# Layer 0: column biases' two row tiles on different output partitions, the tokens' statistics first, and the first unit's preparation last in banks of its own

## The chip, the cores and the metric

One Trainium2 chip, of which the kernel uses one core. A core has TensorE (PE, whose weight loads are listed apart as PEld), VectorE (DVE), ScalarE (ACT), GpSimd (POOL) and SyncE (SP, which only issues transfers). PSUM, where TensorE writes, has 128 partitions and 8 banks of 512 fp32 numbers for each partition; SBUF is the other on-chip memory. The metric is the time of one execution on the device in microseconds; the time of a kernel is the median of its runs. The engines run side by side, each working off its own queue in order; a semaphore holds an instruction until what it reads is there.

## The reference, cut to what matters

Four layers work one after the other on x of shape (2, 64, 64, 128). The change is in layer 0, an attention over all 4096 places of an image with four heads of 32 numbers and a relative position bias by row and by column:

```python
def _gn(v, G=32, eps=1e-5):          # each image, groups of 4 channels
    ...
    return ((g - m) / jnp.sqrt(s + eps)).reshape(v.shape)

def _L0_conv_ref(x, w_qkv, pos_emb_h, pos_emb_w):
    ...
    qkv = jnp.einsum('bhwc,cd->bhwd', x, w_qkv)
    q, k, v = jnp.split(qkv, [qk_dims, 2 * qk_dims], axis=-1)
    ...
    pos = relative_position_bias(pos_q, pos_emb_h, pos_emb_w).reshape(B, nh, L, L)
    scores = jnp.einsum('bnqd,bnkd->bnqk', q, k) * scale + pos
    attn = jax.nn.softmax(scores, axis=-1)
    out = jnp.einsum('bnqk,bnkd->bnqd', attn, v)
    ...

x = x + _L0_conv_ref(_gn(x), L0_conv_w_qkv, L0_conv_pos_emb_h, L0_conv_pos_emb_w)
```

`rel_logits_1d` gives for each query the product with the 64 embeddings of the possible distances in a row (`pos_emb_w`), and the same for columns of the image (`pos_emb_h`). All numbers are fp32. Layers 1 to 3 (a gated triangle product, an attention, two mixtures of experts) are not touched.

## The kernel before, in words

The whole image pair stays in SBUF as `self.x`, 64 blocks of 128 places by 128 channels, 32 blocks (`NC`) for each of the two images (`b`). Eight transfers of 512 KB, all on SP's queue, load it (L51 to L52).

**The start of layer 0** (`layer0`, L257). ACT's queue fetches `w_qkv` (L264) and then the two tables of position embeddings into `raw` (L282). POOL copies one-hot rows into the keys' tile `ka` (`l0_hot`, L499). In the order of the program there follow:

1. The tables: TensorE transposes them (L286), DVE and ACT copy each to four places of `pe` (L289).
2. A bound on the scores, from Gram matrices of the weights (L306, L320), the tables' norms and, later, the longest token: a chain of small DVE and TensorE instructions up to L354.
3. For each image `group_block` eight times (four transposes L113, `bn_stats` on DVE L116, a copy to `xT` on ACT L118), then `group_stats` (L125 to L105: aggregate, two tiny matmuls, a reciprocal root), then `xT` scaled by DVE in two halves (L395).
4. `lengths` for each half image: a Square (on ACT, L375, for the first half and on POOL, L373, for the second), four matmuls (L378), a maximum on DVE (L385). Between them stand `pieces(4)`: four steps of the first unit's preparation each time.
5. The verdict whether the bound is at most 60 (`tops`, L402 to L408, `at_most`, L248), which all engines read for the branch.
6. The rest of the first unit's preparation, and `l0_values` of image 0 (L484 and L491): eight groups of four matmuls, each copied to `v` by ACT.

All PSUM tiles of this part come from one tag, `misc`, with five banks. The tile framework lays down a fixed order for each engine when the program is built; it starts from the order of the program and may bring forward what its own estimate takes for ready.

**The loop** (`l0_bounded`, L503; the branch taken here). There are eight units: image, pair of heads, half of the queries. A unit has 4 query blocks of 512 by 32 key blocks. One turn makes the scores of a key block by four matmuls (L615, eight in the trace, since a matmul on fp32 shows as two records), their exponential on ACT (L623), the values of two turns earlier (L573), and the product with the column biases' exponentials `ew` on DVE (L626). After every second turn `piece()` takes one step of a generator, so a unit has 64 places for steps. In them run the finishing steps of the last query block (`l0_finish`, three steps each) and `l0_prepare` of the next unit. `more()` does the same at other places for the statistics of the next layer. Here the tag `misc` has two banks.

**The preparation of a unit** (`l0_prepare`, L639) is a generator whose every `yield` ends a step:

- queries: two projections (L657) into PSUM, each copied by ACT and DVE to six places of `qa` (L677 to L687); 5 steps for each projection, 10 in all;
- column biases: four groups `g`; in each, eight rows by two row tiles of the array (input partitions 32 to 63 and 96 to 127) make 16 matmuls, 32 records (L701). The right operand is `qa[..., y::S]`, every 64th number. Each row tile has a PSUM bank of its own (`pw[0]`, `pw[1]`), and both write partitions 0 to 63. ACT takes the exponential of each bank (L712) into the lower half of `ew`, and one transfer of 1 MB on SP's queue (L715) copies that to the upper half; 8 steps;
- row biases: four groups of 16 matmuls (L723), two row tiles (input partitions 0 to 31 and 64 to 95) writing partitions 0 to 63 and 64 to 127 of one bank; two copies by ACT and two by DVE for each group (L734); 4 steps;
- in the first half of a pair also the keys: four projections (L657), eight copies by ACT (L747) and eight by DVE (L748); 4 steps.

That is 26 steps for a unit with keys and 22 without.

## Time and profile before

The kernel's time is 4788.5 us (median of 4 runs, 4786.6 to 4790.2). The profiled execution took 4790.6 us, of which 4788.8 are the span from its first to its last instruction.

| stretch, us from the span's start | PE busy | DVE busy | ACT busy | granted clock |
|---|---|---|---|---|
| whole span, 4788.8 | 93% | 61% | 56% | 0.961 |
| start of layer 0, 0 to 88.36 | 55.31 | 44.36 | 49.45 | 0.77 |
| loop of layer 0, 88.36 to 2086.00 | 1959.24 | 1418.19 | 1239.42 | 1.00 |

The rows that the change and its neighbours touch, for the whole span:

| line and engine | instructions | mean or median of one, ns |
|---|---|---|
| L615 PE scores | 8192 | 595 |
| L573 PE values into the output | 8192 | 592 |
| L701 PE column biases | 1024 | 283 |
| L723 PE row biases | 1024 | 217 |
| L491 ACT copies of the values | 16 | 586 |

Busy time is a union of what overlaps: several matmuls on different tiles of the array run at the same time, so that mean times count is more than busy time. An engine's busy share over the whole span says little here, because the start and the loop have different limits; the stretches are to be read one by one. The granted clock is the share of TensorE's full clock that the throttle allowed.

### The profile page before, as it was taken

What the parts mean: (1) busy time and instruction counts of PE and PEld (TensorE: products, weight loads), DVE (VectorE), ACT (ScalarE), POOL (GpSimd) and SP (SyncE); (2) the same over time, 40 slices, a digit from 0 to 9 for tenths busy, and PEclk for the clock granted to TensorE, in tenths of its full rate; (3) what the DMA queues carried; (4) which work ended last, traced back from release to release, by engine and by line L of the source; (5) the groups of instructions that cost most, each with busy time, mean ns of one, the idle gap of its engine ahead of it and who ended that gap; (6) DMA issues with size and microseconds to landing.
All of it is one profiled execution on the core that took longest, in us unless ns stands there. A gap on an engine that the chain in (4) does not pass through costs nothing.

```text
span 4788.8 us, 76270 instructions
## 1 busy us (share of the span) xinstructions
PE 4473.5 (93%) x32236; PEld 1745.9 (36%) x32236; DVE 2943.8 (61%) x4850; ACT 2696.0 (56%) x3157; POOL 945.6 (20%) x848
## 2 busy tenths in 40 slices
PE   6999999999999999977899999999967999999999
PEld 3333333333333333335323233222235444444444
DVE  5676767677766767766755657555564444444447
ACT  5666565656666665545666766676731444333326
POOL 1000000000000000014455555555521000000008
PEclk8999999999999999988999999999977999999999
DMA  1000000000000000000000000000034000000001
GB/s 47 10 1 10 1 10 1 10 1 1 10 1 10 1 12 1 1 5 21 5 1 1 1 1 1 1 1 1 1 109 181 1 0 0 0 1 0 0 1 36
DMA packets 42562, 60.16 MB, mean 13 GB/s; under 512 B 4224, under 2 KB 24928, under 8 KB 41568
## 3 DMA queue, kind: packets, MB, share of 16 engines
q1 hardware_dynamic: 40912, 54.34, 3.7%
q8 instruction: 257, 4.21, 0.4%
q10 hardware_dynamic: 1296, 0.82, 0.1%
q14 instruction: 97, 0.79, 0.1%
HBM read 42.56 MB, written 4.19 MB: 10 GB/s over the span
## 4 chain that ended last, share of the span: by engine, by line
PE 76%; DVE 10%; ACT 7%; issue 3%; POOL 3%; DMA 0%; SPq 0%; ACTq 0%; POOLq 0%; DVEq 0%
PE l0o L573 16%; PE l0sc L615 16%; PE scl L2126 9%; PE oTl L2085 9%; PE l2sc L1498 5%; PE l2pos L1245 5%; PE l2av L1544 3%; PE f3ex L2235 2%; DVE l2es L1518 2%; POOL l2es L1521 2%; ACT l0es L623 2%; ACT l2es L1529 1%; DVE l0es L626 1%; PE l0pw L701 1%; PE l1p L988 1%
## 5 line engine op out<-in xcount | busy, mean ns | idle before, releaser
L626 DVE TENSOR_TENSOR l0es<-l0es,l0qe 128x1024 f32<-128x1024 f32 x1024 | 1250.3, 1228 | 529.4 <-ACT l0es L623 528.3
L623 ACT ACTIVATE l0es<-l0sc 128x1024 f32<-128x1024 f32 x1024 | 1043.3, 1024 | 605.0 <-PE l0sc L615 599.1
L573 PE MATMUL l0o<-l0es,l0v 64*33 64x512 f32 x8192 | 1072.8, 592 | 32.5 <-DVE l0es L626 17.0
L615 PE MATMUL l0sc<-l0qe,ka 64*64 64x512 f32 x8192 | 1079.6, 595 | 5.6 <-ACT l0es L623 5.0
L1529 ACT ACTIVATE l2es<-l2es 128x1024 f32<-128x1024 f32 (+3 forms) x576 | 559.1, 984 | 264.8 <-POOL l2es L1521 257.9
L1521 POOL TENSOR_TENSOR l2es<-l2es 128x1024 f32<-128x1024 f32 (+3 forms) x352 | 581.2, 1662 | 496.8 <-DVE l2es L1518 430.4
L2093 DVE TENSOR_TENSOR accl<-accl,esl 128x1024 f32<-128x1024 f32 x240 | 302.6, 1261 | 424.9 <-ACT esl L2137 421.2
L1518 DVE TENSOR_SCALAR l2es<-l2sc 128x1024 f32<-128x1024 f32 (+3 forms) x320 | 338.9, 1059 | 313.1 <-PE l2sc L1498 312.7
L2137 ACT ACTIVATE esl<-scl 128x1024 f32<-128x1024 f32 x240 | 245.6, 1023 | 485.2 <-PE scl L2126 451.8
L615 PEld LDWEIGHTS l0sc<-l0qe,ka 64*64 64x64 f32 x8192 | 298.5, 133 | 568.0 <-issue 490.2
L573 PEld LDWEIGHTS l0o<-l0es,l0v 64*33 64x33 f32 x8192 | 255.3, 108 | 646.4 <-issue 517.4
L2126 PE MATMUL scl<-l3qT,l3kT 128*128 128x512 f32 x1024 | 487.8, 596 | 0.0
L1498 PE MATMUL l2sc<-l2q,kept 32*128 32x512 f32 (+3 forms) x2304 | 390.9, 621 | 86.8 <-ACT l2es L1509 62.5
L2085 PE MATMUL oTl<-esl,l3v 128*128 128x512 f32 x960 | 451.1, 592 | 0.0
L776 POOL TENSOR_TENSOR x<-x,l0y 128x256 f32<-128x256 f32 x32 | 23.4, 731 | 1994.3 <-DVE l0y L771 1900.0
L1544 PE MATMUL l2av<-l2es,kept 128*32 128x512 f32 (+3 forms) x2304 | 310.0, 588 | 0.0
L1245 PE MATMUL l2pos<-kept 128*32 128x512 f32 x2416 | 296.6, 599 | 0.1
L2126 PEld LDWEIGHTS scl<-l3qT,l3kT 128*128 128x128 f32 x1024 | 188.3, 191 | 207.7 <-issue 191.5
L2085 PEld LDWEIGHTS oTl<-esl,l3v 128*128 128x128 f32 x960 | 181.7, 190 | 225.6 <-issue 222.5
L1509 ACT ACTIVATE l2es<-l2sc 128x1024 f32<-128x1024 f32 x224 | 226.2, 1010 | 54.4 <-PE l2sc L1498 53.0
L1498 PEld LDWEIGHTS l2sc<-l2q,kept 32*128 32x128 f32 x2304 | 116.6, 187 | 331.2 <-ACT l2es L1509 162.7
L1245 PEld LDWEIGHTS l2pos<-kept 128*32 128x32 f32 x2416 | 78.3, 111 | 174.8 <-issue 174.0
(707 smaller groups left out, 3763.2 us busy)
## 6 DMA issues: line engine op xcount, KB each, us to landing
f2w<-in_L_ffn_weight_dram SPq DMA_DIRECT2D x32, 1024.0 KB, 12.9
l0qe<-l0qe SPq DMA_DIRECT2D x8, 1024.0 KB, 6.7
x<-in_x_dram SPq DMA_DIRECT2D x8, 512.0 KB, 8.9
out_dram<-x SPq DMA_DIRECT2D x16, 256.0 KB, 2.3
kept<-in_L_attn_pos_rev_dram SPq DMA_DIRECT2D x1, 1792.0 KB, 6.5
ew<-in_L_ffn_expert_w_dram SPq DMA_DIRECT2D x1, 512.0 KB, 4.1
kept<-in_L_attn_pos_rev_dram SPq DMA_DIRECT2D x1, 256.0 KB
f2b<-in_L_ffn_weight_dram ACTq DMA_DIRECT2D x2, 128.0 KB, 2.8
```

The source lines that it names most:

```text
L573: nc.tensor.matmul(o[64 * h : 64 * h + HD + 1, r, :], lhsT=v1[rows, k, 2 * pair + h, :], rhs=es[rows, h, :], start=(k == 0), stop=(k == NC ...
L615: nc.tensor.matmul(sc[64 * c : 64 * c + 64, h, :], lhsT=ka[rows, k0 : k0 + 64], rhs=qa[rows, k // (NC // 2), qs], start=True, stop=True,)
L623: nc.scalar.activation(es, sc, AF.Exp)
L626: nc.vector.tensor_tensor(es, es, ew[:, :, qs], ALU.mult)
L1245: nc.tensor.matmul(out[part], lhsT=lhsT[:, part], rhs=rhs, start=start, stop=stop)
L1498: nc.tensor.matmul(sc[:, h2, off:], lhsT=kT[hs, k * P : (k + 1) * P], rhs=q[hs, off:], start=True, stop=True,)
L1518: nc.vector.tensor_scalar(es[:, :, lo:], sc[:, :, lo:], root, None, ALU.mult)
L1521: nc.gpsimd.tensor_tensor(part, part, part, ALU.mult)
L1529: nc.scalar.activation(es[:, :, off:], es[:, :, off:], AF.Silu)
L1544: nc.tensor.matmul(avs[i][hs, off:], lhsT=v[:, k, hs], rhs=es[h // 2][:, h % 2, off:], start=(k == 0), stop=last,)
L2085: nc.tensor.matmul(oT, lhsT=vs[b][:, k, :], rhs=es[:, i, :], start=(k == 0), stop=(k == NC - 1),)
L2126: nc.tensor.matmul(sc[:, i, :], lhsT=kTs[b][:, k * P : (k + 1) * P], rhs=qT[:, qb * 512 : (qb + 1) * 512], start=True, stop=True,)
```

## The change

- Two of the eight x transfers, blocks 32 to 47 (the first half of image 1), move from SP's queue to ACT's, where they are issued before `w_qkv`. `raw` moves to the weights' pool, and its two transfers are issued right after `w_qkv`.
- A local function `normed(b)` does the group blocks, the statistics and the scaling of one image. `normed(0)` stands before the tables and the bound, `normed(1)` between the `lengths` of image 0 and of image 1. Image 1's second Square goes from POOL to ACT.
- The first unit's preparation is no longer taken in pieces: it follows whole after the verdict, and it and `l0_values` use a tag `first`. The pool has four banks for each tag, eight in all, instead of five for one.
- In `l0_values` every second copy goes to DVE, for image 1 too, whose values are made inside the loop.
- In `l0_prepare`, for all units, the two row tiles of the column biases write partitions 0 to 63 and 64 to 127 of one bank. The row biases' copies have one more `yield` in each group, and the keys' copies one more in each projection: 34 steps with keys and 26 without.

```diff
@@ -49,7 +49,8 @@
         self.x = self.const.tile([P, B * NC, C], F32, tag="x", name="x")
         src = ins["x"].rearrange("b h w c -> (b h w) c").rearrange("(g p) c -> p g c", p=P)
         for g in range(0, B * NC, 8):
-            nc.sync.dma_start(out=self.x[:, g : g + 8, :], in_=src[:, g : g + 8, :])
+            queue = nc.scalar if g in (NC, NC + 8) else nc.sync
+            queue.dma_start(out=self.x[:, g : g + 8, :], in_=src[:, g : g + 8, :])
 
         self.ident = self.const.tile([P, P], F32, tag="ident", name="ident")
         make_identity(nc, self.ident)
@@ -262,6 +263,10 @@
             wp = st.enter_context(tc.tile_pool(reuse_waits="tile", name="l0w", bufs=1))
             w = wp.tile([P, 3 * C], F32, tag="wqkv", name="wqkv")
             nc.scalar.dma_start(out=w, in_=ins["L0_conv_w_qkv"])
+            raw = wp.tile([P, 2, HD], F32, tag="raw", name="l0raw")
+            nc.vector.memset(raw, 0.0)
+            for i, n in enumerate("hw"):
+                nc.scalar.dma_start(out=raw[: 2 * S - 1, i, :], in_=ins[f"L0_conv_pos_emb_{n}"])
 
 
             pe = wp.tile([P, 2, 2 * S - 1], F32, tag="pe", name="l0pe")
@@ -274,14 +279,18 @@
             v = wp.tile([P, NC, NH, HD + 1], F32, tag="v1", name="l0v1")
             with (
                 tc.tile_pool(reuse_waits="tile", name="l0s", bufs=2) as ap,
-                tc.tile_pool(reuse_waits="tile", name="l0sp", bufs=5, space=PSUM) as ps,
+                tc.tile_pool(reuse_waits="tile", name="l0sp", bufs=4, space=PSUM) as ps,
             ):
-                raw = ap.tile([P, 2, HD], F32, tag="raw", name="l0raw")
-                nc.vector.memset(raw, 0.0)
+                def normed(b):
+                    for g in range(NC // 4):
+                        self.group_block(ps, gst[:, b], b, g, xT[:, b, :])
+                    gm, gr = self.group_stats(ps, gst[:, b], b)
+                    for half in range(2):
+                        part = xT[:, b, half * 2048 : (half + 1) * 2048]
+                        nc.vector.tensor_scalar(part, part, gm, gr, ALU.subtract, ALU.mult)
+
+                normed(0)
                 for i, n in enumerate("hw"):
-                    nc.scalar.dma_start(
-                        out=raw[: 2 * S - 1, i, :], in_=ins[f"L0_conv_pos_emb_{n}"]
-                    )
                     pt = ps.tile([P, 512], F32, tag="misc", name=f"l0pe{n}")
                     nc.tensor.transpose(pt[:HD, :P], raw[:, i, :], self.ident)
                     for lo in range(0, P, 32):
@@ -357,19 +366,10 @@
                 nc.vector.memset(ones, 1.0)
                 most = ap.tile([P, 4], F32, tag="most", name="l0most")
                 nc.vector.memset(v[:, :, :, HD:], 1.0)
-                made = {}
-                first = self.l0_prepare(
-                    ps, (0, 0, 0), xT, w, pe, [ka], (qe[:, 0], qe[:, 1]), made
-                )
-
-                def pieces(n):
-                    for _ in range(n):
-                        next(first, None)
-
                 def lengths(b, half):
                     part = xT[:, b, half * 2048 : (half + 1) * 2048]
                     sq = ap.tile([P, 2048], F32, tag="sq", name=f"l0sq{b}_{half}")
-                    if half:
+                    if half and b == 0:
                         nc.gpsimd.tensor_tensor(sq, part, part, ALU.mult)
                     else:
                         nc.scalar.activation(sq, part, AF.Square)
@@ -387,15 +387,9 @@
                     )
 
                 for b in range(B):
-                    for g in range(NC // 4):
-                        self.group_block(ps, gst[:, b], b, g, xT[:, b, :])
-                    gm, gr = self.group_stats(ps, gst[:, b], b)
+                    if b:
+                        normed(b)
                     for half in range(2):
-                        part = xT[:, b, half * 2048 : (half + 1) * 2048]
-                        nc.vector.tensor_scalar(part, part, gm, gr, ALU.subtract, ALU.mult)
-                for b in range(B):
-                    for half in range(2):
-                        pieces(4)
                         lengths(b, half)
                 top = self.tops(ps, "l0", [most])
                 s1 = self.small.tile([1, 1], F32, tag="bs1", name="l0s1")
@@ -408,9 +402,11 @@
                     s1, s2, float(HD) ** -0.5, s1, ALU.mult, ALU.add
                 )
                 small = self.at_most("l0", s1, 60.0)
-                for _ in first:
+                for _ in self.l0_prepare(
+                    ps, (0, 0, 0), xT, w, pe, [ka], (qe[:, 0], qe[:, 1]), {}, tag="first"
+                ):
                     pass
-                self.l0_values(ps, 0, xT, w, v)
+                self.l0_values(ps, 0, xT, w, v, tag="first")
             with tc.If(small > 0) as fits:
                 self.l0_bounded(xT, w, pe, gst, na, nb, qe, ka, v)
             with fits.Else():
@@ -475,11 +471,11 @@
             nc.tensor.transpose(pt[:, k * P : (k + 1) * P], xT[:, at : at + P], self.ident)
         nc.scalar.activation(xT[:, blk], pt, AF.Identity, bias=nb, scale=na)
 
-    def l0_values(self, ps, b, xT, w, v, ones=False):
+    def l0_values(self, ps, b, xT, w, v, tag="misc"):
 
         nc = self.nc
         for g in range(NC // 4):
-            pv = ps.tile([P, 4, C], F32, tag="misc", name=f"l0pv{b}_{g}_{ones}")
+            pv = ps.tile([P, 4, C], F32, tag=tag, name=f"l0pv{b}_{g}")
             for i in range(4):
                 nc.tensor.matmul(
                     pv[:, i, :],
@@ -488,7 +484,7 @@
                     start=True,
                     stop=True,
                 )
-            nc.scalar.copy(
+            (nc.vector.tensor_copy if g % 2 else nc.scalar.copy)(
                 v[:, 4 * g : 4 * g + 4, :, :HD],
                 pv.rearrange("p i (h d) -> p i h d", d=HD),
             )
@@ -636,7 +632,7 @@
             while extra:
                 more()
 
-    def l0_prepare(self, ps, unit, xT, w, pe, kas, place, made):
+    def l0_prepare(self, ps, unit, xT, w, pe, kas, place, made, tag="misc"):
 
 
 
@@ -652,7 +648,7 @@
 
         def projected(j, g, name):
 
-            out = ps.tile([P, 512], F32, tag="misc", name=name)
+            out = ps.tile([P, 512], F32, tag=tag, name=name)
             for i in range(2):
                 nc.tensor.matmul(
                     out[64 * i : 64 * i + 64, :],
@@ -691,15 +687,12 @@
         for g in range(4):
 
 
-            pw = [
-                ps.tile([P, 8, 2, S // 2], F32, tag="misc", name=f"l0pw{t}_{g}_{i}")
-                for i in range(2)
-            ]
+            pw = ps.tile([P, 8, 2, S // 2], F32, tag=tag, name=f"l0pw{t}_{g}")
             for n in range(8):
                 for i, lo in ((0, 32), (1, 96)):
                     y = 32 * i + 8 * g + n
                     nc.tensor.matmul(
-                        pw[i][:S, n, :, :],
+                        pw[64 * i : 64 * i + S, n, :, :],
                         lhsT=pe[lo : lo + HD, 1, S - 1 - y : 2 * S - 1 - y],
                         rhs=qa[lo : lo + HD, :, y::S],
                         start=True,
@@ -709,13 +702,13 @@
             for i in range(2):
                 y = 32 * i + 8 * g
                 dst = ew[:S].rearrange("p h (x y) -> p y h x", y=S)
-                nc.scalar.activation(dst[:, y : y + 8], pw[i][:S], AF.Exp)
+                nc.scalar.activation(dst[:, y : y + 8], pw[64 * i : 64 * i + S], AF.Exp)
             yield
 
         nc.sync.dma_start(out=ew[S:], in_=ew[:S])
         for g in range(4):
 
-            ph = ps.tile([P, 8, S], F32, tag="misc", name=f"l0ph{t}_{g}")
+            ph = ps.tile([P, 8, S], F32, tag=tag, name=f"l0ph{t}_{g}")
             for i in range(8):
                 row = 8 * g + i
                 at = S - 1 - (half * (S // 2) + row)
@@ -730,6 +723,8 @@
             yield
             cols = slice(g * 512, (g + 1) * 512)
             for lo in (0, 64):
+                if lo:
+                    yield
                 for kh, copy in ((0, nc.scalar.copy), (1, nc.vector.tensor_copy)):
                     copy(
                         qa[lo + 32 : lo + 64, kh, cols].rearrange("p (x y) -> p x y", y=S),
@@ -740,8 +735,8 @@
             root = float(HD) ** -0.5
             for g in range(0, L // 512, 2):
                 pk = projected(1, g, f"l0pk{b}_{pair}_{g}")
-                yield
                 for i in range(2):
+                    yield
                     cols = slice((g + i) * 512, (g + i + 1) * 512)
                     lo = 64 * i
                     nc.scalar.activation(ka[:HD, cols], pk[lo : lo + HD], AF.Copy, scale=root)
```

## The prediction

> **What bounds the kernel now.** I read the page first (TensorE is busy for 93% of the span), then the chain of waits in order of time, the timeline of the first 90 us, the busy time by stretch, and last the column-bias line L701 beside its twin L723. The change touches layer 0 alone, so the span falls in three: the start, up to the first score matmul (L615) at 88.36 us; the loop of eight units, up to about 2086 us; and all the rest, which I take as unchanged.
>
> The loop is bound by TensorE: one turn of 16 score and value matmuls starts every 1.715 us (starts of L615 in the timeline). A prepared piece of the next unit costs the loop only the TensorE time that it inserts. The start is not bound by one engine throughout:
>
> ```profile
> 54.37 2.78 PE l0pw L701 x32
> 59.01 3.73 PE l0pw L701 x64
> 68.23 6.48 PE l0ph L723 x122
> 74.71 4.25 PE l0pk L657 x12
> 81.05 7.40 PE l0pv_False L484 x64
> 91.50 2.22 DVE l0es L626 x2
> ```
> This is the chain (start, length, what). From 54 us the end of the start is set by TensorE, through column biases, row biases, keys and values. Before that it goes from engine to engine, as the timeline shows (start, length, engine, line; in brackets the idle time before):
>
> ```profile
> 18.51 5.93 PE L113 MATMUL gt<-ident,x 128*128 128x128 f32 x32
> 32.96 2.58 DVE L395 TENSOR_SCALAR xT<-xT,gm,gr 128x2048 f32<-128x2048 f32 x2
> 41.73 2.60 DVE L395 TENSOR_SCALAR xT<-xT,gm,gr 128x2048 f32<-128x2048 f32 x2
> 67.41 0.14 DVE L248 TENSOR_SCALAR bok_l<-l0s 1x1 int32<-1x1 f32 x1
> ```
> No token is transposed before 18.5 us, the verdict of the bound (L248) comes at 67.55, and by stretch (window, length, then busy us of PE, PEld, DVE, ACT and POOL, clock, DMA) no engine is full until the last one:
>
> ```profile
> 18.50:44.33 25.83, 18.24 (x89) 14.27 (x88) 19.93 (x44) 13.61 (x24) 3.60 (x1) 0.74 0.03 7
> 44.33:67.55 23.22, 13.64 (x150) 8.15 (x148) 9.75 (x24) 17.77 (x22) 3.60 (x1) 0.63 0.01 2
> 67.55:88.36 20.81, 19.56 (x222) 15.62 (x219) 10.71 (x17) 15.56 (x26) 7.55 (x4) 0.76 0.25 51
> ```
>
> **Part 1, the column biases (L691 to L712).** The 32 matmul records of a group keep their number and sizes; the second row tile now writes partitions 64 to 127 of one bank instead of 0 to 63 of another. The row biases (L723) already have that form: two row tiles, 64 output partitions each, one bank. The tempting sum is to price the new form by L723. By stretch, L701 and then L723:
>
> ```profile
> 60.77:62.74 1.97, 1.97 (x36) 1.77 (x32) 0.50 0.03 8
> 133.79:135.79 2.00, 1.98 (x32) 1.74 (x32) 1.00 0.03 8
> ...
> 436.20:437.37 1.17, 1.15 (x32) 1.01 (x32) 1.00 0.94 196
> ```
> At full clock a group takes 1.98 us against 1.15, so 28 groups in the loop would give 28 x 0.83 = 23 us. I do not take this, for two reasons in the rows. First, the clock: at a granted 0.50 the chain has L723 at 6.48/122 = 53 ns a record and L701 at 3.73/64 = 58; at 1.00 L723 falls to 36 and L701 stays, at 62. If the two tiles of L701 took turns at full clock, then at half clock they would need about twice the 62 ns. They do not, so they already run together, and what holds them does not follow the clock. Second, the operand: L701 streams q by every 64th column (`y::S`), L723 by consecutive ones. A pair of weight loads of one size, strided by 64 and not, shows what that costs (duration in ns: least, median, most):
>
> ```profile
> L988 PEld LDWEIGHTS l1p<-wcat,xT x128: 291/295/333, 2131.6 to 2201.6; 128*128 128x128 f32 x128
> L982 PEld LDWEIGHTS l1pg<-xT,wcat x32: 190/190/333, 2134.3 to 2199.9; 128*128 128x128 f32 x32
> ```
> The strided load (L988) takes 105 ns more. The change leaves the stride. So I take 0 for this part; the bounds are -23 us (L723's price) and +44 (the pairs lose their overlap: twice the 1.98 less some start, +1.57 us, 28 times). The exponentials L712 keep their number and about 1.05 us each.
>
> The Trainium skill, "SBUF — State Buffer" (under "Door 1: The DMA port swizzle"), says that fp32 may be strided for free only within 16 bytes; this stride is 256 bytes, which agrees with L988 and would also make the part worth nothing. A rule that speaks against the edit is in "TensorEngine Tiling (Array Packing)", "Restrictions and Gotchas": different row tiles may not access one PSUM bank at the same time. L723 does so at 36 ns a record, so by the row there is no price; by the rule taken literally it would be the +44 us.
>
> **Part 2, tokens first.** Now the order on TensorE puts the position tables (L286), which wait until 13.2 us for their transfer, and the norm bound behind them, ahead of the tokens. After the change batch 0 goes first. Step by step:
> - The fourth x transfer (batch 0's last) lands at 3.19 + 10.6 = 13.8 us, the sixth at 9.45 + 7.6 = 17.1. With two transfers of batch 1 on ACT's queue, sharing the DMA engines, batch 0 is complete between these: 16. Two groups remain: 8 transposes at 5.93/32 = 0.185, one bn_stats of 0.70: 18.2. From the aggregate to the reciprocal root batch 1 took 37.38 to 41.70, 4.3 us: 22.5. Scaling, 2 x 1.29: 25.1. Before it was 35.5.
> - The tables, Gram matrices and norms (about 4.8 us of DVE in 20 small instructions), batch 1's eight bn_stats (5.6), batch 0's own chain and scaling (4.5) and two reductions (1.4) keep DVE to 18.2 + 16.3 = 34.5. Then 4.3 of chain and 2.6 of scaling: 41.4, against 44.3. Here DVE is the bound, so tokens first earns only 3 us at this point.
> - The second Square of batch 1 moves from POOL (3.60) to ACT (1.91): 43.7. Four length matmuls at low clock 1.94, reduction 0.69, verdict 2.2 (65.36 to 67.55): 48.5 instead of 67.55.
> - Moved transfers: ACT's queue now issues two x transfers ahead of w_qkv, both tables, its table load and its first copy. SP's issues took 0.44 to 3.94 us each, so ACT is held until 2 to 9 us; its first copy needs x, which is not there before about 8. The tables land later than 13.2, perhaps at 17, under batch 0's statistics; if that cover were gone they would cost some 3 us. SP's next loads, of later layers, come earlier, which nobody waits for. POOL loses one Square and has no work behind it.
>
> **Part 3, first unit last, in four banks of its own.** Before, 16 of its 26 pieces stood among the length matmuls (L378 at 57 and 62.7 behind L701). Now all come after the verdict in the program, though the order on an engine may still bring forward what is ready. Its costs: query projection about 2 us; copies L677 to L687, 47.3 to 56.1, 8.8; TensorE 7.4 (four L701 groups) + 6.8 (L723) + 5.2 (keys) + 7.4 (values) = 26.8. One end: nothing is brought forward and TensorE fills nothing: 48.5 + 2 + 8.8 + 26.8 = 86, with a lag or two 89. Other end: projections, copies, keys and values fit in the gaps of the statistics: 41.4 + 4.5 (lengths, verdict) + 14.2 = 60, but ACT then has about 24 us after 41.4: 66. By ACT's rate: after 41.4 it has Squares 2.3, exponentials 8.5, two table loads 2.6, row-bias copies 4.6, key copies 4.7, value copies 2.3 (four of eight now on DVE) and half of the query copies 3.9 = 28.9. From 44.33 to 88.36 it was busy 33.34 of 44.03 us, 76%; at that rate 41.4 + 38 = 79.4. I take 79: **-9.4 us**, between -22 and +1.
>
> **Part 4, pieces and values in the loop.** The extra yields make 26 and 34 pieces of 22 and 26; with 12 of the finishing steps that is at most 46 of 64 places, so no unit becomes late. They thin copies that are hidden today, except where the last key copies meet the end of the second query block: 0.6 + 0.4 us in three units (starts of L615 in units 1, 3 and 5). Between 0 and -3; I take **-1.5**. The values of batch 1 (L484, 64 x 112 ns of TensorE, ACT waiting 0.3 us before each copy) are bound by TensorE; copies on DVE (about 0.69 by L734) do not shorten that: 0, +-0.5.
>
> **Sum.** -9.4 - 1.5 = -10.9 us against the profiled span of 4788.8 (its execution is timed at 4790.6, 2 above the median of 4788.5); against the median 4777.6, told as 4778. A measurement here tells 0.2%, 9.6 us, from no change, so this lies almost on that border.
>
> **Rivals.**
> - A: the column biases do go to L723's 1.15 us: -23 more, 4754. For it: the twin's form. Against it: the half-clock rows and the stride. 10%.
> - B: the start gains nothing: the first unit waits behind the verdict and TensorE's 26.8 us is laid end to end (86 to 89): 4786 to 4789. For it: 19.56 of the last 20.81 us are TensorE now. Against it: four free banks, and keys and values that need only batch 0. 13%.
> - C, slower: two row tiles in one bank take turns: +1.57 us in 28 groups and 4 at the start, +50, so 4828. It decides from 0.65 us a group (32 x 0.65 = 21, which turns -10.9 into +10). Against it: L723 at 1.15. 7%, with any like loss.
>
> **How the numbers follow.** The forecast has 70%: 45 with the start at 78.5 us or earlier, faster by over 0.2%, and 25 within it. A adds 10 to faster; B puts 9 in the same and 4 in slower; C 7 in slower. That is faster 0.55, same 0.34, slower 0.11. The range takes in the forecast's bounds (-22 - 3 and +1: 4763.5 to 4789.5) and reaches towards A: 4757 to 4790.
>
> **What would show it.** L701's groups still at about 1.98 us in the loop (1.15: A; 3.5: C). First transposes L113 near 8 us, L395 of batch 0 ending near 25 and of batch 1 near 41, L248 near 48, first L615 near 79. If L248 is early and L615 not, it is B. I am wrong if the order on the engines puts the first unit's copies ahead of the statistics, so that L248 comes late, or if a transfer on ACT's queue holds up its copies beyond 15 us.

## The result, and the profile after

The changed kernel takes **4794.67 us** (median of 40 runs, 4790.97 to 4797.5) beside 4787.26 for the kernel before (60 runs, 4781.85 to 4792.03): a ratio of **1.0015, 95% interval 1.001 to 1.0019**. It is slower by 7 us. The forecast was 10.9 us faster, and the time lies above its range. The difference is under the 0.2% that was named as the border, so by the prediction's own bound it is "within 0.2%", on the slower side.

The profiled spans are 4788.8 before and 4792.7 after, at granted clocks of 0.961 and 0.964. Cut as the prediction cuts them (the start, up to the first score matmul; the loop of eight units, up to the end of its last score matmul; the rest), they differ by +3.03, +3.93 and -3.04 us. The rest holds nothing that the change touches, and over the fourteen profiles of this study it lies between 2693.5 and 2702.8 us whatever the kernel: its -3 is scatter, and also the reason why the spans differ less than the medians.

| kernel | first transpose | tables in use | first statistics | tokens scaled, image 0 / 1 | verdict | first score | loop | two exponentials, start to start |
|---|---|---|---|---|---|---|---|---|
| before | 18.51 | 13.35 | 19.66 | 35.55 / 44.33 | 67.56 | 88.36 | 1997.60 | 0.855 |
| after | 6.19 | 21.39 | 22.55 | 36.99 / 57.37 | 68.65 | 91.39 | 2001.53 | 1.081 |

(All in us from the span's start, but for the last two columns, which are durations. "Tables in use" is VectorE's first instruction on the position tables, L300 after; "statistics" are the bn_stats, L117; "scaled" is the end of L290; "verdict" the end of L249.)

**The start.** The timeline after, of TensorE and then of VectorE (start, length, engine, line; in brackets the idle time before and what ended it):

```profile
6.19 1.94 PE L114 MATMUL gt<-ident,x 128*128 128x128 f32 x8 [6.19 <-DMA x<-in_x_dram]
9.90 1.97 PE L114 MATMUL gt<-ident,x 128*128 128x128 f32 x8 [1.77 <-DMA x<-in_x_dram]
...
23.92 3.68 PE L114 MATMUL gt<-ident,x 128*128 128x128 f32 x16 [12.05 <-ACT xT L119]
...
21.39 0.23 DVE L300 TENSOR_TENSOR l0posq<-l0raw 128x64 f32<-128x64 f32 x1 [20.18 <-DMA l0raw<-in_L_conv_pos_emb_w_dram]
22.55 2.48 DVE L117 BATCH_NORM_STATS2 gst<-gt 128x6 f32<-128x512 f32 x4
...
42.65 4.87 DVE L117 BATCH_NORM_STATS2 gst<-gt 128x6 f32<-128x512 f32 x8
54.77 2.60 DVE L290 TENSOR_SCALAR xT<-xT,gm,gr 128x2048 f32<-128x2048 f32 x2
```
The transposes do start 12 us earlier, as announced. But after 16 of them TensorE stops for 12 us. VectorE, which should read the statistics of what was transposed, is idle until 21.39, and what ends its 20.18 us of idle time is the transfer of a position table. L300, the first step of the norm bound, stands ahead of every bn_stats in VectorE's queue. In the program it comes after `normed(0)`; the framework's order for VectorE put it first. The four groups that were transposed fill the four banks, and no bank comes free until the table is there. The chain of waits (start, length, what) says the same in one line, and shows what delays image 1 later on:

```profile
4.38 0.53 ACTq L269
4.94 16.32 DMA l0raw<-in_L_conv_pos_emb_w_dram
...
37.18 3.69 POOL l0sq L373
40.91 1.11 PE l0n L378 x8
42.04 0.69 DVE l0most L385
42.73 4.79 DVE gst L117 x8
47.55 0.43 DVE l0qe L682
48.00 0.38 DVE gmv L126
```
The table's transfer is issued at 4.9 us behind 1 MB of tokens on ACT's queue and lands at 21.3; before it was in use at 13.35. From 37 us on the statistics of image 1 wait for a length of image 0, whose Square is on GpSimd, and then they share VectorE with the first unit's query copies (L682 here).

From the scaling of image 1 (57.37) to the verdict (68.65) it takes another 11.3 us. TensorE's timeline shows why:

```profile
54.05 6.28 PE L694 MATMUL l0pw<-l0qe,l0pe 32*64 32x64 f32 x94 [2.74 <-ACT l0qe L683]
60.26 1.94 PE L378 MATMUL l0n<-l0sq,l0ones 128*32 128x512 f32 x8
62.13 1.80 PE L694 MATMUL l0pw<-l0qe,l0pe 32*64 32x64 f32 x28
63.85 1.93 PE L378 MATMUL l0n<-l0sq,l0ones 128*32 128x512 f32 x8
```
The first unit's column biases (L694) were brought forward, ahead of image 1's length matmuls (L378) and of the verdict, although in the program they follow it. VectorE waits 4.89 and 2.90 us for these lengths.

**The tail of the start and the loop.** By stretch (window, length, then busy us of PE, PEld, DVE, ACT and POOL, clock, DMA), from the verdict to the first score, and one group of column biases in the loop:

```profile
68.65:91.39 22.74, 20.17 (x188) 14.69 (x186) 12.62 (x19) 16.03 (x25) 7.55 (x4) 0.70 0.23 48
```
```profile
402.05:404.10 2.05, 1.98 (x32) 1.74 (x32) 1.00 0.00 0
```
The tail lasted 20.81 us before and lasts 22.74 now, 20.17 of it on TensorE. The column biases cost 1.98 us a group, as before (1.97 in the median of the 28 groups). What changed in the loop is on ACT. The timeline of ACT round one group's two exponentials, before and then after:

```profile
390.89 1.95 ACT L712 ACTIVATE l0qe<-l0pw 64x512 f32<-64x512 f32 x2 [1.71 <-PE l0pw L701]
392.64 2.11 ACT L623 ACTIVATE l0es<-l0sc 128x1024 f32<-128x1024 f32 x2
```
```profile
394.88 2.13 ACT L705 ACTIVATE l0qe<-l0pw 64x512 f32<-64x512 f32 x2 [1.72 <-PE l0pw L694]
397.04 1.94 ACT L619 ACTIVATE l0es<-l0sc 128x1024 f32<-128x1024 f32 x2
```
One exponential lasts about 1.05 us in both kernels. Before, the second starts 0.855 us after the first, so the two overlap and take 1.95; after, it starts 1.081 us later and the pair takes 2.13. The loop's own exponential stands behind them and comes 0.4 us later: 2.16 us after the pair's start instead of 1.75. Before, it too started while the pair was still running; after, it does not.

### The profile page after: what moved, and what is told of

The parts are those of the page before. It is cut to its first block, busy times and chain, and to the rows that moved or that the text cites. A ratio compares the mean times of both kernels' runs of the same rounds, so it can differ in the third digit from the quotient of the medians.

```text
span 4792.7 us, 76262 instructions
## 1 busy us (share of the span) xinstructions
PE 4469.3 (93%) x32236; PEld 1733.8 (36%) x32236; DVE 2947.9 (62%) x4858; ACT 2701.0 (56%) x3150; POOL 943.1 (20%) x847
## 2 busy tenths in 40 slices
DMA packets 42562, 60.16 MB, mean 13 GB/s; under 512 B 4224, under 2 KB 24928, under 8 KB 41568
## 4 chain that ended last, share of the span: by engine, by line
PE 76%; DVE 10%; ACT 7%; issue 3%; POOL 3%; DMA 1%; ACTq 0%; SPq 0%; POOLq 0%; DVEq 0%
PE l0o L569 16%; PE l0sc L611 15%; PE scl L2121 9%; PE oTl L2080 9%; PE l2sc L1493 5%; PE l2pos L1240 5%; PE l2av L1539 3%; PE f3ex L2230 2%; DVE l2es L1513 2%; POOL l2es L1516 2%; ACT l0es L619 1%; ACT l2es L1524 1%; DVE l0es L622 1%; PE l0pw L694 1%; PE l1p L983 1%
## 5 line engine op out<-in xcount | busy, mean ns | idle before, releaser
L622 DVE TENSOR_TENSOR l0es<-l0es,l0qe 128x1024 f32<-128x1024 f32 x1024 | 1249.9, 1228 | 521.2 <-ACT l0es L619 519.9
L619 ACT ACTIVATE l0es<-l0sc 128x1024 f32<-128x1024 f32 x1024 | 1040.4, 1024 | 605.1 <-PE l0sc L611 595.3
```

What stands on the lines that cost most here:

```text
L619: nc.scalar.activation(es, sc, AF.Exp)
L622: nc.vector.tensor_tensor(es, es, ew[:, :, qs], ALU.mult)
```

## Experiments: the start

**Tables first** takes the changed kernel and puts the two small transfers and w_qkv ahead of the two x transfers on ACT's queue. It tells a wait for the tables from a start that TensorE alone bounds.

```diff
-            queue = nc.scalar if g in (NC, NC + 8) else nc.sync
-            queue.dma_start(out=self.x[:, g : g + 8, :], in_=src[:, g : g + 8, :])
+            if g not in (NC, NC + 8):
+                nc.sync.dma_start(out=self.x[:, g : g + 8, :], in_=src[:, g : g + 8, :])
...
                 nc.scalar.dma_start(out=raw[: 2 * S - 1, i, :], in_=ins[f"L0_conv_pos_emb_{n}"])
+            nc.scalar.dma_start(out=w, in_=ins["L0_conv_w_qkv"])
+            src = ins["x"].rearrange("b h w c -> (b h w) c").rearrange("(g p) c -> p g c", p=P)
+            for g in (NC, NC + 8):
+                nc.scalar.dma_start(out=self.x[:, g : g + 8, :], in_=src[:, g : g + 8, :])
```

> The changed kernel, with the two position tables and w_qkv fetched ahead of image 1's x blocks on ACT's queue. Theory (the first DVE instruction of the norm bound stands ahead of all bn_stats on DVE's queue and waits for the tables, which land at 21.3 us behind 1 MB of x): the tables land by 7 us, the first bn_stats starts near 8 instead of 22.55, image 0 is scaled near 27 instead of 37, the first score matmul comes near 82 instead of 91.4, and the time falls by 8 to 10 us to about 4785, ratio to the kernel before about 0.9995. Rival (the first unit's preparation behind the verdict sets the end, whatever the statistics do): first score matmul still at 89 to 91, ratio about 1.0015.

Measured: 4785.2 us, ratio to before 0.9997 (0.9988 to 1.0006). VectorE's timeline:

```profile
13.37 0.23 DVE L303 TENSOR_TENSOR l0posq<-l0raw 128x64 f32<-128x64 f32 x1 [12.16 <-DMA l0raw<-in_L_conv_pos_emb_w_dram]
14.53 3.22 DVE L117 BATCH_NORM_STATS2 gst<-gt 128x6 f32<-128x512 f32 x5
```
The tables come 8.0 us earlier (13.37 for 21.39), the statistics 8.0, the verdict 7.7 (60.94) and the first score 7.7 (83.68): the wait is handed on almost whole to the end of the start. That the tables' landing sets the start is thereby shown. The loop stays at 2001.32. The two tables of 16 KB are there only at 13.3 us, as in the kernel before, and not by 7 as expected, and VectorE still waits 12 us for them; as built, the 192 KB of w_qkv stand ahead of them on the queue.

## Experiments: the two exponentials

Three kernels separate "one bank" from "other partitions". **Two banks** gives the changed kernel the old form of the output, with the rest of the change left in:

```diff
-            pw = ps.tile([P, 8, 2, S // 2], F32, tag=tag, name=f"l0pw{t}_{g}")
+            pw = [ps.tile([P, 8, 2, S // 2], F32, tag=tag, name=f"l0pw{t}_{g}_{i}") for i in range(2)]
...
-                        pw[64 * i : 64 * i + S, n, :, :],
+                        pw[i][:S, n, :, :],
...
-                nc.scalar.activation(dst[:, y : y + 8], pw[64 * i : 64 * i + S], AF.Exp)
+                nc.scalar.activation(dst[:, y : y + 8], pw[i][:S], AF.Exp)
```

> The changed kernel, with the column biases' row tiles again in two banks on partitions 0 to 63. Theory (two exponentials that read one bank start 1.08 us apart instead of 0.855, which costs the loop 0.3 us in each of 28 groups): start to start 0.855 again, the loop 6 to 8 us shorter than the changed kernel's 2001.5, the groups of column biases still 1.98 us; ratio about 1.0000. Rival (the extra steps and the value copies on DVE make the loop longer): loop still 2001.5, ratio about 1.0015.

**One bank** is the reverse edit on the kernel before, so that this part of the change stands alone:

```diff
-            pw = [ps.tile([P, 8, 2, S // 2], F32, tag="misc", name=f"l0pw{t}_{g}_{i}") for i in range(2)]
+            pw = ps.tile([P, 8, 2, S // 2], F32, tag="misc", name=f"l0pw{t}_{g}")
...
-                        pw[i][:S, n, :, :],
+                        pw[64 * i : 64 * i + S, n, :, :],
...
-                nc.scalar.activation(dst[:, y : y + 8], pw[i][:S], AF.Exp)
+                nc.scalar.activation(dst[:, y : y + 8], pw[64 * i : 64 * i + S], AF.Exp)
```

> The kernel before, with only the column biases' outputs changed: one bank, partitions 0 to 63 and 64 to 127. Theory: groups stay at 1.98 us, exponentials 1.08 us apart, loop longer by 28 x 0.3 = 8 us, ratio about 1.0017. Rival (the loop's loss comes from the other edits): ratio 1.0000. If the row tiles had taken turns before, groups would fall to 1.15 us and the ratio to 0.995.

**Two banks, shifted** is the kernel before with the second tile still in a bank of its own, but on partitions 64 to 127 of it:

```diff
-                        pw[i][:S, n, :, :],
+                        pw[i][64 * i : 64 * i + S, n, :, :],
...
-                nc.scalar.activation(dst[:, y : y + 8], pw[i][:S], AF.Exp)
+                nc.scalar.activation(dst[:, y : y + 8], pw[i][64 * i : 64 * i + S], AF.Exp)
```

> The kernel before, with two banks kept and the second row tile's output on partitions 64 to 127 of its own bank. If the exponentials lose their overlap because they read one bank: 0.855 us apart as before, ratio 1.0000. If they lose it because the second reads other partitions than it writes: 1.08 us apart, loop 8 us longer, ratio 1.0017.

| kernel | median | ratio (95%) | loop | group of column biases | exponentials, start to start |
|---|---|---|---|---|---|
| before | - | 1 | 1997.60 | 1.97 | 0.855 |
| after | 4794.67 | 1.0015 (1.001 to 1.0019) | 2001.53 | 1.97 | 1.081 |
| two banks | 4784.62 | 0.9996 (0.9987 to 1.0005) | 1998.29 | 1.97 | 0.855 |
| one bank | 4790.05 | 1.0009 (1.0 to 1.0018) | 2001.97 | 1.97 | 1.081 |
| two banks, shifted | 4793.57 | 1.0011 (1.0002 to 1.002) | 2004.00 | 1.97 | 1.079 |

ACT's timeline in the last of them and in "two banks":

```profile
392.09 2.14 ACT L712 ACTIVATE l0qe<-l0pw 64x512 f32<-64x512 f32 x2 [1.70 <-PE l0pw L701]
```
```profile
391.83 1.93 ACT L708 ACTIVATE l0qe<-l0pw 64x512 f32<-64x512 f32 x2 [1.70 <-PE l0pw L697]
```
I had put the longer pair down to the shared bank, and that was a miss: with a bank for each tile, but the second on partitions 64 to 127, the pair takes 2.14 us and the loop is the longest of the five. What the three slow cases share is that the second exponential reads partitions 64 to 127 and writes partitions 0 to 63, and the fast ones do not. In the loop the other partitions cost 3.2 us (after less two banks), 4.4 (one bank less before) and 6.4 (shifted less before). Each loop is read from one profile, but kernels with the same loop agree: tables first lies 0.21 us from the changed kernel, the fast start below 0.03 from "two banks". The length of each unit, from the starts of the score matmuls, shows why the three sums differ (us; unit 7 prepares nothing and changes by 0.01):

| difference | units 0 to 3 and 6, each | unit 4 | unit 5 | loop |
|---|---|---|---|---|
| after less two banks | 1.19 to 1.23 | -3.33 | 0.54 | 3.24 |
| one bank less before | 1.23 to 1.26 | -2.40 | 0.54 | 4.37 |
| shifted less before | 1.08 to 1.13 | 0.30 | 0.52 | 6.40 |

In five of the units each of the four groups makes one turn about 0.3 us longer, in all three comparisons. Unit 4, in which the next layer's first statistics run too, falls short of that sum by 0.9 to 4.5 us, depending on the kernel; what it gains there is not traced.

"Two banks" also ends its start 1.84 us earlier (89.55 for 91.39). Of the 10 us by which its median lies below that of the changed kernel, start and loop hold 5.1; the remainder is in the part that no edit touches. The eleven times of "two banks, shifted" lie from 4785.9 to 4787.9 and from 4793.6 to 4795.7, none between, so its median says little, and the loop in its profile decides. The runs show which partitions matter, not why the engine then starts later, nor whether reading 64 to 127 is enough by itself, since no run also writes there.

## Experiments: the stride

**Turned queries** store the queries of layer 0 transposed, so that the column biases read 32 consecutive columns instead of every 64th. Four of the copies then write every 32nd column. It was put on the kernel before and on the kernel after, so both forms of the output are priced without the stride.

```diff
-                    (nc.scalar.copy if h else nc.vector.tensor_copy)(right[0], right[1])
+                    (nc.scalar.copy if h else nc.vector.tensor_copy)(
+                        turned(96, h)[:, :, S // 2 :], rows(p)[:, :, S // 2 :]
+                    )
...
-                        rhs=qa[lo : lo + HD, :, y::S],
+                        rhs=qa[lo : lo + HD, :, 32 * y : 32 * y + 32],
```

> The kernel before, with the queries for the column biases written transposed, so that L701 reads 64 consecutive numbers instead of every 64th; outputs as before, two banks, partitions 0 to 63. One more small ACT copy for each query block. If the stride alone holds the groups at 1.98 us: 1.15 us as the row biases, loop about 20 to 23 us shorter, ratio 0.995 to 0.996. If the shared output partitions hold them: still 1.98 us, ratio 1.000 or a little more.

> The changed kernel with the same transposed queries; one bank, partitions 0 to 63 and 64 to 127. If the stride alone counts: groups 1.15 us, exponentials still 1.08 us apart, loop 2001.5 - 23 = 1978, ratio about 0.9965. If stride and output partitions each hold the groups: 1.15 here and 1.98 in the kernel before with the same edit.

Measured: 4827.38 us, ratio 1.0086 (1.0072 to 1.0099), and 4834.42, ratio 1.0101 (1.0086 to 1.0117). One group by stretch, first on the kernel before, then on the kernel after:

```profile
144.70:146.10 1.40, 1.15 (x32) 1.01 (x32) 1.00 0.00 0
```
```profile
148.90:150.30 1.40, 1.15 (x32) 1.01 (x32) 1.00 0.00 0
```
The group falls from 1.98 to 1.15 us in both, to the price of the row biases. So the stride held the matmuls, and the output's partitions play no part: in neither form did they make the two tiles take turns. The Trainium skill, "SBUF — State Buffer" (under "Door 1: The DMA port swizzle"), allows fp32 a free stride only within 16 bytes; this pair agrees with it, and puts 0.83 us a group on a stride of 256 bytes. The rule of "TensorEngine Tiling (Array Packing)", "Restrictions and Gotchas", against two row tiles in one PSUM bank found no price here: 1.15 us with one bank and with two.

The time got worse all the same: the loop took 2031.54 and 2038.95 us, 34 and 37 more, although 28 x 0.83 = 23 us of matmuls were saved. The groups' turns are 0.8 us shorter each, and the turns with the query projections lose more than that. The groups of instructions show where, before and then turned (busy us, mean ns of one; idle before):

```profile
L686 ACT COPY l0qe<-l0pq 32x256 f32<-32x256 f32 x28 | 10.2, 363 | 14.0 <-DVE l0qe L686 13.2
```
```profile
L684 ACT COPY l0qe<-l0pq 32x256 f32<-32x256 f32 x28 | 16.8, 598 | 19.6 <-DVE l0qe L684 19.3
```
The strided stores take 598 ns instead of 363, and the copies of one projection wait for each other in turn, ACT for VectorE and back. The loop's exponentials stand behind them: the score matmuls (L615) waited 5.0 us in all for ACT's exponentials in the loop before and wait 47.9 now, most of the 57 us that the turning cost (34 lost although 23 were saved).

## Experiments: the yields, and a faster version

**Yields alone**: the kernel before with the change's yields and nothing else: one among the row-bias copies, one more among the key copies.

```diff
             for lo in (0, 64):
+                if lo:
+                    yield
...
-                yield
                 for i in range(2):
+                    yield
```

> The kernel before with only the additional steps in the row biases' and the keys' copies. Theory: the end of the keys' copies no longer meets the end of a query block, about 1 us less in each of units 1, 3 and 5, loop 1994 to 1995, ratio 0.9993 to 0.9998. Rival (the steps do nothing): loop 1997.6.

Measured: 4781.95 us, ratio 0.9992 (0.9983 to 1.0001), so the time alone shows no change. The loop fell from 1997.60 to 1995.91. "Two banks" has the same loop but for one edit, every second copy of image 1's values on VectorE, and it takes 1998.29: 2.38 us more, all of it in unit 4, where those values are made (2.46, of which 1.3 in two of its first six turns; every other unit agrees within 0.12). So the value copies on VectorE cost more than the yields had saved.

**Turned, with all that was learnt** is the changed kernel with two banks, turned queries, and the tables on SP's queue ahead of x (the order as built has one x transfer first):

```diff
+        self.raw = self.const.tile([P, 2, HD], F32, tag="raw", name="l0raw")
+        nc.vector.memset(self.raw, 0.0)
+        for i, n in enumerate("hw"):
+            nc.sync.dma_start(out=self.raw[: 2 * S - 1, i, :], in_=ins[f"L0_conv_pos_emb_{n}"])
...
-                nc.scalar.dma_start(out=raw[: 2 * S - 1, i, :], in_=ins[f"L0_conv_pos_emb_{n}"])
+            raw = self.raw
```

> The changed kernel with two banks on partitions 0 to 63, transposed queries, and the two tables fetched on SP's queue ahead of x. Theory: tables before 7 us, first bn_stats near 8, first score matmul near 80, loop 1998.3 - 23 = 1975, time about 4754, ratio 0.993. If the tables still land at 13 us, first score matmul near 83; if the transposing copies cost the loop more than they save, loop above 1990.

**Turning on GpSimd** has the kernel before turn the queries with GpSimd copies from the SBUF, so that neither ACT nor VectorE does it:

```diff
+                        nc.gpsimd.tensor_copy(
+                            qa[lo : lo + HD, h, :].rearrange("p (y x) -> p x y", x=S // 2)[:, xs, ys],
+                            qa[64 * h : 64 * h + HD, 0, cols].rearrange("p (x y) -> p x y", y=S)[:, :, ys],
+                        )
```

> The kernel before, with L701's queries transposed by POOL from the copies in SBUF, instead of by ACT and DVE from PSUM; ACT and DVE lose three small copies for each query block. If the loss of the first transposed version was the chain of ACT and DVE copies on one PSUM bank, and not the transposed operand: groups 1.15 us, loop 1997.6 - 28 x 0.82 = 1974 or less, ratio about 0.995. Rival (POOL's copies come late, or slow DVE down): loop above 1990.

**Fast start** is the changed kernel with two banks and the tables on SP's queue, and no turning.

> The changed kernel with two banks on partitions 0 to 63 and the two tables on SP's queue ahead of all but the first x transfer; no transposed queries. Both causes of the loss are undone: tables at 10.9 us, first score matmul near 82, loop 1998, ratio about 0.9985. If the start is held by something else than the tables: first score matmul at 87 or later, ratio 0.9996 as with two banks alone.

**Both** is the fast start with the turning on GpSimd; **both, spread** adds three empty yields to each query projection, so that its steps lie further apart.

> The same with POOL's transposed queries: first score matmul near 83, loop 1975, time about 4757, ratio about 0.9935. Rival as for the kernel before with POOL's copies.

> As best_pool, with three more empty steps in each query projection, so that ACT's 1.00 us copy and the next block's copy fall into different places of the loop. If what ate the 0.82 us gain of each group was ACT's copies standing two to a step: loop about 1985 instead of 1996.8, time about 4765, ratio about 0.9955. If POOL's copies themselves slow DVE: loop still about 1995, ratio 0.998 as best_fast or worse.

| kernel | median | ratio (95%) | tables in use | tokens scaled, 0 / 1 | verdict | first score | loop |
|---|---|---|---|---|---|---|---|
| turned, all | 4826.19 | 1.0086 (1.0073 to 1.01) | 10.86 | 28.35 / 48.75 | 59.54 | 87.24 | 2038.30 |
| turning on GpSimd | 4788.53 | 1.0004 (0.9995 to 1.0013) | 13.23 | 34.3 / 43.1 | 70.20 | 90.63 | 1997.88 |
| fast start | **4776.38** | **0.9979 (0.997 to 0.9988)** | 11.20 | 28.15 / 48.32 | 57.83 | 80.67 | 1998.26 |
| both | 4779.9 | 0.9985 (0.9976 to 0.9994) | 11.06 | 28.49 / 46.82 | 60.16 | 80.28 | 1996.81 |
| both, spread | 4782.06 | 0.9991 (0.9982 to 1.0) | 11.22 | 28.44 / 46.78 | 60.12 | 80.27 | 1999.71 |

"Turned, all" keeps the loss of the turned loop and so missed its 4754 us.

**The fast start beats both kernels**, by 10 us the one before and by 18 the changed one. VectorE's timeline, with the first score:

```profile
11.20 0.22 DVE L303 TENSOR_TENSOR l0posq<-l0raw 128x64 f32<-128x64 f32 x1 [9.98 <-DMA l0raw<-in_L_conv_pos_emb_w_dram]
...
25.56 2.60 DVE L293 TENSOR_SCALAR xT<-xT,gm,gr 128x2048 f32<-128x2048 f32 x2
...
33.80 4.87 DVE L123 BATCH_NORM_STATS2 gst<-gt 128x6 f32<-128x512 f32 x8
```
Image 0 is scaled at 28.15, 3 us from the 25.1 of the prediction. Image 1 is at 48.32, later than before the change (44.33), since its statistics still stand behind image 0's lengths. From the verdict to the first score it is 22.84 us, as after.

GpSimd's turning breaks even in the loop although each group saves 0.83 us: in most units one or two turns with a projection in them cost 2.1 to 2.6 us more. The groups of instructions in "turning on GpSimd" over the loop, and last the score matmuls of the kernel before:

```profile
L683 POOL COPY l0qe<-l0qe 32x256 f32<-32x256 f32 x112 | 80.9, 723 | 166.9 <-DVE l0qe L675 163.0
```
```profile
L677 ACT COPY l0qe<-l0pq 32x1024 f32<-32x1024 f32 x28 | 28.1, 1003 | 31.0 <-DVE l0qe L675 31.0
L615 PE MATMUL l0sc<-l0qe,ka 64*64 64x512 f32 x8192 | 1084.0, 598 | 22.7 <-ACT l0es L623 22.7
```
```profile
L615 PE MATMUL l0sc<-l0qe,ka 64*64 64x512 f32 x8180 | 1078.3, 595 | 5.6 <-ACT l0es L623 5.0
```
ACT's last query copy (L677) waits 31.0 us in all for VectorE's copy, and the score matmuls wait 22.7 us for the exponentials that stand behind it on ACT, instead of 5.0. That is most of what the groups save. The GpSimd copies themselves cost VectorE little: of the 36 products (L626) beside one, 28 took more than 1.3 us instead of 1.23, but over all 1024 products the mean rose only from 1228 to 1234 ns, 6 us in the loop. Spreading the steps did not bring it back: the same waits are 31.5 and 24.4 us.

## Why the prediction was wrong, point by point

**Part 1** was right in its own claim: 0 us, since the stride and not the output form holds the matmuls. The groups stayed at 1.97 to 1.98 us, and both turned kernels confirm the reason. What failed is its last sentence, "The exponentials L712 keep their number and about 1.05 us each". They do, and still the pair takes 0.2 us more: I priced them by their duration, and the trace of before already showed two starts 0.855 us apart, an overlap that could be lost. That overlap is worth 3.2 to 6.4 us of loop. Of the two reasons given for the 0 us, the stride is confirmed. The one from the half clock is weaker than it reads: it takes twice the time for granted there, where L723's own rows went from 36 to 53 ns.

**Part 2** failed at "The tables land later than 13.2, perhaps at 17, under batch 0's statistics; if that cover were gone they would cost some 3 us". There was no cover: the work named as hiding the wait stood behind it in VectorE's queue. The tables landed at 21.3, VectorE idled for 20.18 us, and the three terms that follow (25.1, 41.4 and 48.5) all went with it: 36.99, 57.37 and 68.65. Tables first shows 8 us of it; the fast start shows 8.8 of the 11.9 us that image 0 was late (28.15 for 36.99, where the sum had 25.1). The prediction named this among its ways to fail, "if a transfer on ACT's queue holds up its copies beyond 15 us", but looked to ACT's copies and not to VectorE's first instruction. The other way that it named came true too: query copies of the first unit stand among image 1's statistics, and from the aggregate (48.00) to the scaling (54.77) it took 6.8 us where 4.3 was assumed. With the wait for image 0's length this keeps image 1 at 48.32 even in the fast start, 7 us behind the sum. The third bullet failed as well: from the scaling of image 1 to the verdict it sums 7.1 us of lengths, reduction and verdict, and it took 11.3 (9.5 in the fast start), because the column biases that were to move behind the verdict ran ahead of it.

**Part 3** forecast the first score at 79. The changed kernel has it at 91.39, the fast start at 80.67. That the latter is close is partly two errors that cancel: the verdict came 9 us later than summed (57.83 for 48.5) and the tail took 22.8 us where the sum leaves 30.5. In the changed kernel the 12.4 us between forecast and result are +16.0 up to the scaling of image 1, +4.2 from there to the verdict and -7.8 in the tail, which no longer held the column biases. Rival B, a start that gains nothing because the first unit waits behind the verdict and TensorE's work is laid end to end, names the nearest time, 4786 to 4789, and TensorE is busy for most of this tail. But its cause is not what happened: the column biases ran before the verdict, and the start moved with the verdict, earlier whenever the tables came earlier.

**Part 4** was right about the yields: -1.5 forecast, -1.69 in the loop with the yields alone. The two turns behind the second query block that it meant became 1.1 us shorter in units 1 and 3, though not in unit 5. It was wrong about the values: "copies on DVE (about 0.69 by L734) do not shorten that: 0, +-0.5", and they cost 2.4 us, the difference of "two banks" and "yields alone". Rival A fell with the stride, as argued against it, and rival C's price per group did not appear in any run. C's sign came true by another mechanism, on ACT.

The sum then reads: start +3.0 in place of -9.4; loop +3.9, of which the yields give -1.7, the value copies on VectorE +2.4 and the exponentials +3.2 (taken from "one bank", in the other order, the copies +1.2 and the exponentials +4.4).

## What to carry to other kernels

Work hides a wait only if it can be issued while the wait lasts: before calling a transfer covered, look which instruction on the consuming engine's queue reads it and what stands behind that one. Moving loads forward on a queue moves others back; a small table that opens a chain belongs ahead of the bulk (here at 11 to 13 us instead of 21). Price two like instructions in a row from start to start, not by their durations, and price the copies that would make an operand contiguous before paying for them.

## What the runs showed of the hardware that was not expected

- Two exponentials from PSUM in a row started 0.855 us apart when each read and wrote partitions 0 to 63, and 1.08 us apart when the second read 64 to 127 and wrote 0 to 63, with one bank or with two. The 128-partition exponential behind the pair started 0.91 us after the second in the first case and 1.08 in the other.
- fp32 matmuls of 32x64 with a moving operand of 256 bytes' stride took 62 ns a record (1.98 us for 32) and 36 (1.15 us) without.
- Copies of 32x256 with strided stores took 598 ns on ACT instead of 363.
- VectorE products of 128x1024 that overlapped a GpSimd copy took 1.15 to 1.53 us, 28 of 36 more than 1.3; with no such copy beside them the median was 1.23.
- The two tables of 16 KB were there at 13.3 us behind 192 KB of w_qkv on ACT's queue, at 11.2 on SP's behind one x transfer, and at 21.3 behind 1 MB of x.
